# An attention and expert block on one core: gaps between score slots laid out anew, and maxima added to the queries by GpSimd

## The chip, the cores and the metric

The kernel runs on one core of a Trainium2 chip. The metric is the device time of one execution in microseconds (us), as the median of several runs. A core has a matrix engine (TensorE, PE in the profile; its weight loads are shown apart as PEld), a vector engine (VectorE, DVE), a scalar engine (ScalarE, ACT), a general engine (GpSimd, POOL) and a synchronising engine (SyncE, SP), which here issues most of the DMAs. Matmuls write to PSUM, a small memory that ACT and DVE read; everything else is kept in SBUF.

## The reference

The input x is 32 sequences of 512 tokens with 256 channels. The block is an attention with 16 heads of 16 channels, a norm, a layer of experts and another norm.

```
q, k = split(x @ W_attn + b_attn);  v = x, cut into heads
y    = causal_attn(q, k, v)
e    = v[1:] - y[:-1]                    # what the first attention missed
k2   = x[:-1] @ W_k2 + b_k2;  q2 = q[1:]
y2   = causal_attn(q2, k2, e), shifted by one token, first row 0
x1   = layernorm(x + proj(y) + proj(y2))
out  = layernorm(x1 + experts(x1))
```

The experts act on 512 tokens alone, those of the first sequence: two of eight experts each, a gated unit of width 256 and a down projection. For the other 31 sequences the second norm follows the first directly.

## The kernel before

**Groups and steps.** The attention is cut into groups of four heads of one sequence, 4 groups a sequence, 128 in all (`n_all`). `step(n)` works on several groups at once, each at another stage: it takes the row maxima of group n, makes scores and exponentials of group n-2 (first attention, a = 0) and of group n-3 (second attention, a = 1), and values and normalizations of groups n-2 and n-3. The PE queue runs in exactly this order (`manual_schedule`); the other engines' instructions are placed by the framework.

**Slots.** A step has five slots (`units` for the maxima, `banks` for the scores). In a slot, for each of two pairs of heads, `scores` writes one PSUM tile `sc` (L265) and `maxima` one tile `sm` for the other pair (L206, L219), so that the two occupy different rows of the array and overlap. `maxima` first adds a mask: four bf16 matmuls per head (`pick` times `hide`, L206) with 128, 96, 64 and 32 columns in each block, one block in units 0 and 3, two in units 1, 2 and 4; then the products of queries and keys in f32 (L219; each such matmul stands in the trace as two passes). DVE reduces each `sm` to maxima (L230) into one of two `mx` buffers. ACT turns each `sc` into exponentials `pt` (L274, 1024 columns), and GpSimd clears the upper triangle of its diagonal blocks (L278).

**Gaps.** Between slots stand other jobs, by the lists `rest[0]` to `rest[4]` (L493 to L539), run after the slot of that number:

- `augment(n-1)`: transposes the maxima (`mt`, L236); DVE adds them to the queries into `qm` (L240), which the scores of group n-1 read from the next step on.
- `normalize(n-3, 0)` and `normalize(n-3, 1)`: transposes (`yt`, L304), then a maximum with a tiny number, a reciprocal and a product on DVE (L308 to L324), then GpSimd (L321 or L325).
- `values(n-3, 1)` and `values(n-2, 0)`: `av`, L289, over the four key blocks j, then a copy by ACT to `avs` (L297).
- `project(two, m)`: for two groups at once q (m = 0), k (m = 1) or k2 (m = 2): `pj`, L169; ACT adds the bias and writes `pk` (L173); eight DMAs on SP move it into `q_t` or `kk_t` (L184). `pk` has two tags, `half0` and `half1`, with one buffer each.
- once a sequence, `turn` (`ys`, L355, copied by ACT to `ysT`) and `attended` for two halves (`po`, L367, added by DVE to `h`, L374). From the second sequence on `twice_normed` follows on DVE and GpSimd (L389 to L396), and with the second half the store of `h`.

Steps 10 to 17 also carry the experts (`hidden`, `down`).

**PSUM.** All these jobs take their tiles by `bank2` from one pool of four buffers of two banks (L61). They go round in the order in which they are asked for: a tile can be written when the tile four places earlier has been read.

Of the kernel before, what the change touches and what calls it, by code (L numbers as in the profile page):

```python
# [8 lines left out]
F32 = mybir.dt.float32  # L9
# [6 lines left out]
P = 128  # L16
HD = 16
HS = 32
GH = 4
# [8 lines left out]
def block_kernel(  # L28
# [16 lines left out]
    nc = tc.nc  # L45
    B, T, C = x.shape
    NB = T // P
    NC = C // P
    NG = C // (GH * HD)
    E = w_gu.shape[0]  # L50
# [9 lines left out]
    small = ctx.enter_context(tc.tile_pool(name="small", bufs=4))  # L60
# [136 lines left out]
    def maxima(n, u, pair):  # L197
        d = groups[n]
        parts, first, step, kinds = units[u]
        ps = bank2(f"sm{n}_{u}_{pair}")  # L200
        blocks = ps.rearrange("p h (k c) -> p h k c", c=P)
        heads = [(hh, slice(HS * (NH2 * pair + hh), HS * (NH2 * pair + hh + 1))) for hh in range(NH2)]

        for c in range(NB):
            for hh, rows in heads:
                nc.tensor.matmul(  # L206
                    blocks[:, hh, first::step, HS * c :],
                    pick[rows, c],
                    hide[rows, c, kinds[0] : kinds[1], HS * c :],
                    start=(c == 0),  # L210
                    stop=False,
                )
        for i, a, na, at in parts:
            nk = (i + 1) * P
            view = ps[:, :, at * P : at * P + na * nk].rearrange("p h (a k) -> p h a k", k=nk)
            order = [slice(i * P, nk), slice(0, i * P)] if i else [slice(0, P)]
            for keys in order:
                for hh, rows in heads:
                    nc.tensor.matmul(  # L219
                        view[:, hh, :, keys],  # L220
                        d["q"][rows, i * P : (i + 1) * P],
                        d["kk"][rows, a : a + na, keys],
                        start=False,
                        stop=(at == parts[-1][3] and keys == order[-1]),
                    )
        for i, a, na, at in parts:
            nk = (i + 1) * P
            view = ps[:, :, at * P : at * P + na * nk].rearrange("p h (a k) -> p h a k", k=nk)
            to = mx[n % 2][:, i, NH2 * pair : NH2 * (pair + 1), HD + a : HD + a + na]
            nc.vector.tensor_reduce(to, view, AX.X, ALU.max)  # L230

    def augment(n):
        d = groups[n]
        ps = bank2(f"mt{n}")
        for i in range(NB):
            nc.tensor.transpose(  # L236
                ps[:, 0, i * P : (i + 1) * P], mx[n % 2][:, i].rearrange("p h s -> p (h s)"), ident
            )
        d["qm"] = grp.tile([P, T], F32, tag="qm", name=f"qm{n}")
        nc.vector.tensor_add(d["qm"], ps[:, 0], d["q"])  # L240

# [38 lines left out]
    def values(n, a):  # L282
        b, g = divmod(n, NG)
        d = groups[n]
        vals = (v_pad, e_pad)[a]
        ps = bank2(f"av{n}_{a}")
        for j in range(NB):
            for h in range(GH):
                nc.tensor.matmul(  # L289
                    ps[HS * h : HS * (h + 1), 0, j * P :],  # L290
                    vals[:, j, g * GH + h, :],
                    d["pt", a, j, h // NH2][:, h % NH2],
                    start=(j == 0),
                    stop=(j == NB - 1),
                )
        avs = d["avs", a] = work.tile([P, T], F32, tag="avs", name=f"avs{n}_{a}")
        nc.scalar.copy(avs, ps[:, 0])  # L297

    def normalize(n, a):
        b, g = divmod(n, NG)  # L300
        d, s = groups[n], seqs[b]
        ps = bank2(f"yt{n}_{a}")
        for i in range(NB):
            nc.tensor.transpose(ps[:, 0, i * P : (i + 1) * P], d["avs", a][:, i * P : (i + 1) * P], ident)  # L304
        got = ps[:, 0].rearrange("p (n h s) -> p n h s", h=GH, s=HS)
        den = small.tile([P, NB, GH], F32, tag="den", name=f"den{n}_{a}")

        nc.vector.tensor_scalar_max(den, got[:, :, :, HD], 1e-30)  # L308
        rden = small.tile([P, NB, GH], F32, tag="rden", name=f"rden{n}_{a}")
        nc.vector.reciprocal(rden, den)  # L310
        rb = rden.unsqueeze(3).to_broadcast([P, NB, GH, HD])
        cols = slice(g * GH * HD, (g + 1) * GH * HD)

        def heads(t):
            return t[:, :, cols].rearrange("p n (h d) -> p n h d", d=HD)

        if a == 0:
            if g == 0:
                s["y"] = seq.tile([P, NB, C], F32, tag="y", name=f"y{b}")
            nc.vector.tensor_mul(heads(s["y"]), got[:, :, :, 0:HD], rb)  # L320
            nc.gpsimd.tensor_sub(e_pad[:, :, g * GH : (g + 1) * GH, 0:HD], heads(s["xs"]), heads(s["y"]))  # L321
        else:
            y2 = work.tile([P, NB, GH * HD], F32, tag="y2", name=f"y2_{n}")
            nc.vector.tensor_mul(y2.rearrange("p n (h d) -> p n h d", d=HD), got[:, :, :, 0:HD], rb)  # L324
            nc.gpsimd.tensor_add(s["y"][:, :, cols], s["y"][:, :, cols], y2)  # L325
            groups.pop(n)
# [31 lines left out]
    def attended(b, half):  # L358
        s = seqs[b]
        if half == 0:  # L360
            pool = seq if b else const
            s["h"] = pool.tile([P, NB, C], F32, tag="h" if b else "h0", name=f"h{b}")
        ps = bank2(f"po{b}_{half}")
        two = slice(2 * half, 2 * half + 2)
        for i in range(2):
            for c in range(NC):
                nc.tensor.matmul(  # L367
                    ps[:, 0, i * C : (i + 1) * C],
                    s["ysT"][:, c, (2 * half + i) * P : (2 * half + i + 1) * P],
                    wp_sb[:, c],  # L370
                    start=(c == 0),
                    stop=(c == NC - 1),
                )
        nc.vector.tensor_add(  # L374
            s["h"][:, two], ps[:, 0].rearrange("p (i c) -> p i c", c=C), s["xr"][:, two]
        )
        if b:
            twice_normed(b, half)
        elif half:
            norm(s["h"], f"a{b}")  # L380
# [107 lines left out]


    n_all = B * NG  # L490
    first_expert = 2 * NG + 2

    def step(n):  # L493
        ready = lambda k: 0 <= k < n_all
        rest = [[] for _ in units]
        b, r = divmod(n, NG)
        if r == 1 and b + 1 < B:
            load(b + 1)
        if r == 3 and b + 1 < B:
            load_next(b + 1)  # L500
        if ready(n):
            prepare(n)
        if ready(n - 1):
            rest[0].append(lambda: augment(n - 1))
        if ready(n - 3):
            rest[0].append(lambda: normalize(n - 3, 0))
            rest[3].append(lambda: values(n - 3, 1))
            rest[4].append(lambda: normalize(n - 3, 1))
        two = n // 2 + 1
        if ready(2 * two):  # L510
            for m, s in [(0, 4)] if n % 2 == 0 else [(1, 1), (2, 4)]:
                rest[s].append(lambda m=m: project(two, m))
        if ready(n - 2):
            rest[4].append(lambda: values(n - 2, 0))
        b, r = divmod(n - 4, NG)
        if r == NG - 1 and 0 <= b < B:
            rest[2].append(lambda: turn(b))
        b2, r2 = divmod(n - 5, NG)
        if r2 == NG - 1 and 0 <= b2 < B:
            rest[1].append(lambda: attended(b2, 0))  # L520
            rest[2].append(lambda: attended(b2, 1))
        e = n - first_expert
        if e == -1:
            rest[4] += [route, turn_tokens, lambda: load_expert(0)]
        if 0 <= e < E:
            if e + 1 < E:
                load_expert(e + 1)
            rest[1].append(lambda: hidden(e, 0))
            rest[2].append(lambda: hidden(e, 1))
            rest[4].append(lambda: down(e))  # L530
        if e == E:
            rest[4].append(lambda: second_norm(0, moe["acc"]))
        for s in range(len(units)):
            for pair in range(2):
                scores(n - 2, s, 1 - pair)
                if ready(n):
                    maxima(n, s, pair)
            for f in rest[s]:
                f()  # L539
# [2 lines left out]
    load_next(0)  # L542
    for m in range(3):
        project(0, m)
    for n in range(max(n_all + 5, first_expert + E + 1)):
        step(n)


# [71 lines left out]
```

## Time and profile before

| | |
|---|---|
| median of 3 runs | 3240.24 us (3235.77 to 3241.64) |
| the profiled execution: time, span | 3252.37 us, 3250.7 us |
| granted TensorE clock, mean | 0.986 |
| DVE reduces, L230 | 1792 of 916 ns, 1573.6 us |
| ACT exponentials, L274 | 1282 of 1023 ns, 1297.3 us |
| GpSimd selects, L278 | 2048 of 408 ns, 793.1 us |
| ACT copies of av, L297 | 256 of 586 ns |
| ACT pk, L173 | 192 of 688 ns |
| DVE add to qm, L240 | 128 of 680 ns |

Times in the profile are of one execution. A group's line gives its engine, the operation, what it writes and reads, how many there are, their busy time and mean, and the idle time of the engine just before them with what ended it. Since matmuls are pipelined and overlap, the starts of successive matmuls tell more than their durations. [...]

### The profile page before, as it was taken

What the parts mean: (1) busy time and instruction counts of PE and PEld (TensorE: products, weight loads), DVE (VectorE), ACT (ScalarE), POOL (GpSimd) and SP (SyncE); (2) the same over time, 40 slices, a digit from 0 to 9 for tenths busy, and PEclk for the clock granted to TensorE, in tenths of its full rate; (3) what the DMA queues carried; (4) which work ended last, traced back from release to release, by engine and by line L of the source; (5) the groups of instructions that cost most, each with busy time, mean ns of one, the idle gap of its engine ahead of it and who ended that gap; (6) DMA issues with size and microseconds to landing.
All of it is one profiled execution on the core that took longest, in us unless ns stands there. A gap on an engine that the chain in (4) does not pass through costs nothing.

```text
span 3250.7 us, 98094 instructions
## 1 busy us (share of the span) xinstructions
PE 3159.7 (97%) x42312; PEld 2147.1 (66%) x42312; DVE 1999.3 (62%) x3120; ACT 1668.7 (51%) x1823; POOL 1373.8 (42%) x2847
## 2 busy tenths in 40 slices
PE   5999998999999999999999999999999999999997
PEld 4665555667666666666666666676767676676673
DVE  4664444566666666666666666666666666666662
ACT  2554344455555555555555555555555555555554
POOL 4333334344444344444444444444344444443444
PEclk8999999999999999999999999999999999999998
DMA  4111111111111111111111111111111111111110
GB/s 110 37 28 47 37 48 35 39 50 51 32 50 51 41 51 50 50 46 39 50 44 47 50 50 50 39 44 50 40 51 51 49 51 33 50 48 43 38 28 20
DMA packets 144241, 148.13 MB, mean 46 GB/s; under 512 B 40984, under 2 KB 108992, under 8 KB 143808
## 3 DMA queue, kind: packets, MB, share of 16 engines
q1 hardware_dynamic: 143296, 141.42, 16.0%
q8 instruction: 333, 5.46, 0.7%
q14 instruction: 100, 0.82, 0.1%
q10 hardware_dynamic: 416, 0.39, 0.0%
q0 software_dynamic: 96, 0.04, 0.0%
HBM read 74.63 MB, written 16.78 MB: 28 GB/s over the span
## 4 chain that ended last, share of the span: by engine, by line
PE 88%; POOL 5%; DVE 2%; ACT 2%; issue 1%; SPq 1%; DMA 1%; POOLq 0%; DVEq 0%; ACTq 0%
PE sm L219 28%; PE av L289 18%; PE sc L265 14%; PE pj L169 10%; PE sm L206 5%; PE yt L304 4%; POOL h L396 2%; PE mt L236 2%; PE po L367 2%; POOL pt L278 1%; PE gu L450 1%; PE ys L355 1%; PE dn L473 1%; ACT pt L274 1%; POOL r L393 1%
## 5 line engine op out<-in xcount | busy, mean ns | idle before, releaser
L230 DVE TENSOR_REDUCE mx<-sm 128x2 f32<-128x1024 f32 (+3 forms) x1792 | 1573.6, 916 | 965.2 <-PE sm L219 933.0
L274 ACT ACTIVATE pt<-sc 128x1024 f32<-128x1024 f32 (+1 forms) x1282 | 1297.3, 1023 | 683.7 <-PE sc L265 633.6
L219 PE MATMUL sm<-kk_t,q_t 32*128 32x128 f32 (+2 forms) x12288 | 1431.4, 360 | 13.2 <-DMA kk_t<-pk 13.2
L265 PE MATMUL sc<-qm,kk_t 32*128 32x256 f32 (+3 forms) x8192 | 1369.1, 444 | 1.4 <-DVE mx L230 1.2
L278 POOL TENSOR_SCALAR_AFFINE_SELECT pt<-pt 128x256 f32<-128x256 f32 x2048 | 793.1, 408 | 1256.2 <-ACT pt L274 1255.2
L219 PEld LDWEIGHTS sm<-kk_t,q_t 32*128 32x128 f32 x12288 | 920.7, 188 | 35.4 <-issue 8.5
L265 PEld LDWEIGHTS sc<-qm,kk_t 32*128 32x128 f32 x8192 | 711.1, 185 | 224.9 <-issue 134.6
L206 PE MATMUL sm<-hide,pick 32*128 32x128 bf16 (+5 forms) x10240 | 512.3, 217 | 3.8 <-ACT pt L274 3.4
L206 PEld LDWEIGHTS <-pick 32*128 32x128 bf16 x10240 | 368.8, 93 | 32.0 <-issue 12.3
L169 PE MATMUL pj<-xT,wq_sb 128*128 128x512 f32 x768 | 369.7, 604 | 19.8 <-DMA xT<-in_xT 19.8
L297 ACT COPY avs<-av 128x512 f32<-128x512 f32 x256 | 150.1, 586 | 453.3 <-PE av L289 453.3
L289 PE MATMUL av<-pt,e_pad 128*32 128x512 f32 (+3 forms) x4096 | 315.4, 449 | 24.3 <-ACT pt L274 17.2
L289 PE MATMUL av<-pt,v_pad 128*32 128x512 f32 (+3 forms) x4096 | 303.9, 437 | 4.8 <-POOL pt L278 4.8
L173 ACT ACTIVATE pk<-pj,bp_qk 128x512 f32<-128x512 f32 x192 | 132.0, 688 | 337.2 <-PE pj L169 316.4
L289 PEld LDWEIGHTS av<-pt,e_pad 128*32 128x32 f32 x4096 | 134.2, 112 | 243.2 <-issue 139.8
L289 PEld LDWEIGHTS av<-pt,v_pad 128*32 128x32 f32 x4096 | 120.0, 110 | 248.9 <-issue 115.0
L169 PEld LDWEIGHTS pj<-xT,wq_sb 128*128 128x128 f32 x768 | 131.5, 191 | 121.7 <-issue 93.9
L304 PE MATMUL yt<-ident,avs 128*128 128x128 f32 x1024 | 161.4, 280 | 3.8 <-DVE mx L230 2.9
L321 POOL TENSOR_TENSOR e_pad<-xs,y 128x256 f32<-128x256 f32 x128 | 93.4, 730 | 151.2 <-DVE y L320 151.1
L396 POOL TENSOR_SCALAR h<-h,mv,r 128x256 f32<-128x256 f32 x124 | 150.8, 1223 | 6.5
L367 PE MATMUL po<-wp_sb,ysT 128*128 128x256 f32 x512 | 131.4, 401 | 5.7 <-ACT pt L274 4.6
L325 POOL TENSOR_TENSOR y<-y,y 128x256 f32<-128x256 f32 x128 | 93.9, 734 | 90.6 <-DVE y L324 90.6
(76 smaller groups left out, 1405.5 us busy)
## 6 DMA issues: line engine op xcount, KB each, us to landing
kk_t<-pk SPq DMA_DIRECT2D x1024, 32.0 KB
xT<-in_xT SPq DMA_DIRECT2D x32, 512.0 KB
x<-in_x SPq DMA_DIRECT2D x32, 512.0 KB
q_t<-pk SPq DMA_DIRECT2D x512, 32.0 KB
xr<-in_x SPq DMA_DIRECT2D x32, 512.0 KB
out<-h SPq DMA_DIRECT2D x31, 512.0 KB
xs<-in_x SPq DMA_DIRECT2D x32, 384.0 KB
gu<-in_w_gu SPq DMA_DIRECT2D x8, 512.0 KB
```

Of the source, the lines that this page charges most:

```text
L169: nc.tensor.matmul(ps[:, 0], wq_sb[:, m, c, half * P : (half + 1) * P], seqs[b]["xT"][:, c], start=(c == 0), stop=(c == NC - 1))
L206: nc.tensor.matmul(blocks[:, hh, first::step, HS * c :], pick[rows, c], hide[rows, c, kinds[0] : kinds[1], HS * c :], start=(c == 0), stop ...
L219: nc.tensor.matmul(view[:, hh, :, keys], d["q"][rows, i * P : (i + 1) * P], d["kk"][rows, a : a + na, keys], start=False, stop=(at == part ...
L230: nc.vector.tensor_reduce(to, view, AX.X, ALU.max)
L265: nc.tensor.matmul(ps[:, hh, at * P : at * P + nq], d["kk"][rows, a, j * P : (j + 1) * P], d["qm"][rows, j * P :], start=True, stop=True,)
L274: nc.scalar.activation(pt[:, :, lo:hi], ps[:, :, lo:hi], AF.Exp, scale=HD**-0.5)
L278: nc.gpsimd.affine_select(diag, diag, pattern=[[0, NH2], [1, P]], compare_op=ALU.is_ge, fill=0.0, base=-a, channel_multiplier=-1)
L289: nc.tensor.matmul(ps[HS * h : HS * (h + 1), 0, j * P :], vals[:, j, g * GH + h, :], d["pt", a, j, h // NH2][:, h % NH2], start=(j == 0), ...
L297: nc.scalar.copy(avs, ps[:, 0])
L304: nc.tensor.transpose(ps[:, 0, i * P : (i + 1) * P], d["avs", a][:, i * P : (i + 1) * P], ident)
L367: nc.tensor.matmul(ps[:, 0, i * C : (i + 1) * C], s["ysT"][:, c, (2 * half + i) * P : (2 * half + i + 1) * P], wp_sb[:, c], start=(c == 0) ...
L396: nc.gpsimd.tensor_scalar(t[:, i], t[:, i], mv[:, k, 0:1], r[:, k : k + 1], ALU.subtract, ALU.mult)
```

## The change

- In `maxima` the mask matmuls run in the order of blocks 0, 3, 2, 1, that is with 128, 32, 64, 96 columns.
- `augment` goes from the gap after slot 0 to that after slot 3. ACT copies the transposed maxima out of PSUM, and GpSimd adds the queries in place.
- `values` takes its key blocks in the order 0, 2, 1, 3 for a = 0 and 0, 1, 3, 2 for a = 1.
- `normalize` for a = 0 leaves out the maximum with 1e-30.
- `project`: m = 1 after slot 2 of even steps, m = 0 after slot 1 and m = 2 after slot 2 of odd steps (before: m = 0 after slot 4 of even steps, m = 1 after slot 1 and m = 2 after slot 4 of odd steps). The rule for the tag of `pk` is not touched.
- `attended`: the first half after slot 2 of step n, the second after slot 0 of step n+1 (before: after slots 1 and 2 of step n).
- The first expert comes one step later, and the loop has one step more.

```diff
--- before.py
+++ after.py
@@ -201,7 +201,7 @@
         blocks = ps.rearrange("p h (k c) -> p h k c", c=P)
         heads = [(hh, slice(HS * (NH2 * pair + hh), HS * (NH2 * pair + hh + 1))) for hh in range(NH2)]
 
-        for c in range(NB):
+        for c in (0, *range(NB - 1, 0, -1)):
             for hh, rows in heads:
                 nc.tensor.matmul(
                     blocks[:, hh, first::step, HS * c :],
@@ -237,7 +237,8 @@
                 ps[:, 0, i * P : (i + 1) * P], mx[n % 2][:, i].rearrange("p h s -> p (h s)"), ident
             )
         d["qm"] = grp.tile([P, T], F32, tag="qm", name=f"qm{n}")
-        nc.vector.tensor_add(d["qm"], ps[:, 0], d["q"])
+        nc.scalar.copy(d["qm"], ps[:, 0])
+        nc.gpsimd.tensor_add(d["qm"], d["qm"], d["q"])
 
 
 
@@ -284,14 +285,15 @@
         d = groups[n]
         vals = (v_pad, e_pad)[a]
         ps = bank2(f"av{n}_{a}")
-        for j in range(NB):
+        order = [0, 2, 1, 3] if a == 0 else [0, 1, 3, 2]
+        for j in order:
             for h in range(GH):
                 nc.tensor.matmul(
                     ps[HS * h : HS * (h + 1), 0, j * P :],
                     vals[:, j, g * GH + h, :],
                     d["pt", a, j, h // NH2][:, h % NH2],
-                    start=(j == 0),
-                    stop=(j == NB - 1),
+                    start=(j == order[0]),
+                    stop=(j == order[-1]),
                 )
         avs = d["avs", a] = work.tile([P, T], F32, tag="avs", name=f"avs{n}_{a}")
         nc.scalar.copy(avs, ps[:, 0])
@@ -303,11 +305,14 @@
         for i in range(NB):
             nc.tensor.transpose(ps[:, 0, i * P : (i + 1) * P], d["avs", a][:, i * P : (i + 1) * P], ident)
         got = ps[:, 0].rearrange("p (n h s) -> p n h s", h=GH, s=HS)
-        den = small.tile([P, NB, GH], F32, tag="den", name=f"den{n}_{a}")
-
-        nc.vector.tensor_scalar_max(den, got[:, :, :, HD], 1e-30)
         rden = small.tile([P, NB, GH], F32, tag="rden", name=f"rden{n}_{a}")
-        nc.vector.reciprocal(rden, den)
+        sums = got[:, :, :, HD]
+        if a:
+
+            den = small.tile([P, NB, GH], F32, tag="den", name=f"den{n}")
+            nc.vector.tensor_scalar_max(den, sums, 1e-30)
+            sums = den
+        nc.vector.reciprocal(rden, sums)
         rb = rden.unsqueeze(3).to_broadcast([P, NB, GH, HD])
         cols = slice(g * GH * HD, (g + 1) * GH * HD)
 
@@ -488,7 +493,7 @@
 
 
     n_all = B * NG
-    first_expert = 2 * NG + 2
+    first_expert = 2 * NG + 3
 
     def step(n):
         ready = lambda k: 0 <= k < n_all
@@ -501,14 +506,14 @@
         if ready(n):
             prepare(n)
         if ready(n - 1):
-            rest[0].append(lambda: augment(n - 1))
+            rest[3].append(lambda: augment(n - 1))
         if ready(n - 3):
             rest[0].append(lambda: normalize(n - 3, 0))
             rest[3].append(lambda: values(n - 3, 1))
             rest[4].append(lambda: normalize(n - 3, 1))
         two = n // 2 + 1
         if ready(2 * two):
-            for m, s in [(0, 4)] if n % 2 == 0 else [(1, 1), (2, 4)]:
+            for m, s in [(1, 2)] if n % 2 == 0 else [(0, 1), (2, 2)]:
                 rest[s].append(lambda m=m: project(two, m))
         if ready(n - 2):
             rest[4].append(lambda: values(n - 2, 0))
@@ -517,8 +522,10 @@
             rest[2].append(lambda: turn(b))
         b2, r2 = divmod(n - 5, NG)
         if r2 == NG - 1 and 0 <= b2 < B:
-            rest[1].append(lambda: attended(b2, 0))
-            rest[2].append(lambda: attended(b2, 1))
+            rest[2].append(lambda: attended(b2, 0))
+        b3, r3 = divmod(n - 6, NG)
+        if r3 == NG - 1 and 0 <= b3 < B:
+            rest[0].append(lambda: attended(b3, 1))
         e = n - first_expert
         if e == -1:
             rest[4] += [route, turn_tokens, lambda: load_expert(0)]
@@ -542,7 +549,7 @@
     load_next(0)
     for m in range(3):
         project(0, m)
-    for n in range(max(n_all + 5, first_expert + E + 1)):
+    for n in range(max(n_all + 6, first_expert + E + 1)):
         step(n)
```

## The prediction

> **What bounds the kernel now.** I read the page first, then the waits, then the timeline of one undisturbed stretch. The page's first part and its costliest matmul line say TensorE:
>
> ```profile
> PE 3159.7 (97%) x42312; PEld 2147.1 (66%) x42312; DVE 1999.3 (62%) x3120; ACT 1668.7 (51%) x1823; POOL 1373.8 (42%) x2847
> L219 PE MATMUL sm<-kk_t,q_t 32*128 32x128 f32 (+2 forms) x12288 | 1431.4, 360 | 13.2 <-DMA kk_t<-pk 13.2
> ```
>
> The waits of PE between 640 and 3190 us, after the experts, sum to 0.6 us in three lines. So what an edit changes must be a matmul's own time, or a delay inside a slot, where two pairs of heads overlap and a late start leaves no idle mark. The starts of `mt`, one per step, are at 1622.53, 1645.71, 1667.17, 1691.16 and 1716.07: steps of 23.18, 21.46, 23.99 and 24.91 us, 93.54 for four, and the period repeats to 0.01 us. I call them A, B, C, D (n mod 4 = 1, 2, 3, 0; A and C odd).
>
> Inside a slot the sm tile of the first pair runs, then sc of the other pair starts together with the second sm: two sm chains in a row set its length. After a long gap slots take 2.37 (units 0, 3) and 2.60 to 2.63 us (1, 2, 4). Slot 1 takes 3.14 in A, C and D. The timelines of DVE and PE in B show why:
>
> ```profile
> 1644.70 2.36 DVE L230 TENSOR_REDUCE mx<-sm 128x2 f32<-128x1024 f32 x2 [3.65 <-PE sm L219]
> 1646.97 0.68 DVE L240 TENSOR_TENSOR qm<-mt,q_t 128x512 f32<-128x512 f32 x1
> 1647.57 0.17 DVE L308 TENSOR_SCALAR den<-yt 128x16 f32<-128x16 f32 x1
> ...
> 1648.06 0.42 DVE L320 TENSOR_TENSOR y<-yt,rden 128x256 f32<-128x256 f32 x1
> ```
>
> ```profile
> 1646.74 0.70 PE L265 MATMUL sc<-qm,kk_t 32*128 32x512 f32 x2
> 1647.11 0.37 PE L206 MATMUL sm<-hide,pick 32*128 32x256 bf16 x4
> ```
>
> Four PSUM tiles go round in the order of allocation. The sm tile at 1647.11 takes the place of slot 0's last, whose reduce ended at 1647.06; the second sm waits for `yt`, read until 1648.48. By such comparison the slots lose 0.76, 0.95, 0.55 and 0.52 us in A to D, 2.78 per four steps, some 89 us in all. That is all that moving gaps can win.
>
> [...]the first L219 of a chain takes 0.35 us against 0.27 for its like, for its load begins only with the last, 27 ns long, L206. [...]Here the semaphore moves 1.37 us after the end of the last issue (median of 192 batches). [...]here 1309 ns (L464, 128x512) against 680 (L240).
>
> **The change, part by part.**
>
> Order of the pick matmuls. With widths 128, 32, 64, 96 the last[...] is a wide one. In units 1, 2, 4 (two blocks) starts were 117, 80, 54 ns apart, then 109 to the load's end; now 117, 27, 54, 109: 53 saved. In units 0, 3: 63, 41, 27, 109 become 63, 25, 27, 109: 16 saved. Two chains a slot: 2 x (3 x 53 + 2 x 16) = 382 ns a step, on PE's path, 48.9 us over 128 steps.
>
> Gap after slot 0. `mt` (0.49) and the qm add leave; `yt` stays, 0.53. Now slot 1's first sm waits for the exp of slot 0's second sc, which ends 0.88 after slot 0 (1646.59 against 1645.71): a loss of 0.37 in B, C, D. In A the moved `po` (1.9) covers it.
>
> Slots 1 and 2 adjoin in B and D: DVE needs 2 x (0.96 + 0.42) per slot, PE now 2.5. Stepping the ring through gives 0.20 and 0.17 more, 0.74 each. Slot 3 has a projection before it and loses nothing. Slot losses become 0 + 0.74 + 0.37 + 0.74 = 1.85.
>
> Gaps. PE's work in them is the same, but runs between slots go from 17 to 18 per four steps and neighbours change; adding the pieces (0.53, 1.91, 1.81, 1.02, 2.82 and so on) gives 40.76 against 40.29. Sum: 4 x (12.59 - 0.38) + 1.85 + 40.76 = 91.45, or 2.09 less per four steps; over 31.25 such periods 65 us gained.
>
> Evictions. `qm` costs ACT a copy (586 ns by L297) and GpSimd 1309 ns; both sit in the gap after slot 3 (2.82 with av), 5 us before scores read qm. Should that cover fail, each us late costs PE one, but I find 2.5 to spare. Behind GpSimd's add stand the selects of slot 4, which values reads; by L278 they end 1.6 after slot 4, and with `yt` and j = 0, 2 first, values asks for j = 1 at 1.8. Order of j, the dropped max (164 ns), two more waits of av: nothing, between 0 and 0.1 us a step.
>
> The projections. m=0 and m=2 of one `two` write the same single pk buffer, tag half of (two+m)%2. Before, a step lay between them. Now m=0 stands after slot 1, m=2 after slot 2 of an odd step; m=2's ACTIVATE must wait until eight DMAs have read m=0's pk. ACT and SP in the middle, and the only place where before met this wait, its start (ACT and SP):
>
> ```profile
> 1617.98 0.69 ACT L173 ACTIVATE pk<-pj,bp_qk 128x512 f32<-128x512 f32 x1 [1.66 <-PE pj L169]
> ```
>
> ```profile
> 1618.69 4.93 SPq L184 DMA_DIRECT2D q_t<-pk  x8
> ```
>
> ```profile
> 25.41 0.69 ACT L173 ACTIVATE pk<-pj,bp_qk 128x512 f32<-128x512 f32 x1 [1.08 <-PE pj L169]
> 35.28 0.69 ACT L173 ACTIVATE pk<-pj,bp_qk 128x512 f32<-128x512 f32 x1 [9.19 <-DMA q_t<-pk]
> ```
>
> From the start of m=0's ACTIVATE: 0.71 to the first issue, 5.39 for eight (mean for q_t; 4.93 is the least), 1.37 to land: 7.5. PE brings m=2 there after 1.91 + 2.49 = 4.40. So ACT stands 3.1 us; queued behind are ysT in C, two exps, the qm copy and avs. PE goes on for three tiles; the fourth, slot 3's second sm, reuses pj's bank. It had about 0.3 to spare (ACTIVATE ends 2.71 after pj's start, the sm is due 3.05), so PE loses 2.75. In A, SP's order puts the store of h before these DMAs; h now comes from the po after slot 0: DVE till 4.3 after that slot, GpSimd 3.5 more (L392 to L396), store at 7.9, ACTIVATE's end at 7.6. With 0.4 for the issue, 0.7 more: 3.45. Over 31 periods 192 us, less 8 where `gu` lies between (four odd expert steps, 1.9 each): 184. Bounds: with least issue span and no store 2.3 each, 140; with the issue hiccups of over 1 us, 240. I take the mean since every issue counts.
>
> The clock. In these stops PE is idle 1.6 to 2.4 us. Among the experts it has such stops already; the windows view shows what follows (last columns of interest: PE busy first, PEclk after the five engines):
>
> ```profile
> 268.00:272.70 4.70, 2.21 (x27) 1.08 (x21) 3.56 (x5) 4.37 (x5) 2.32 (x2) 1.00 0.38 112
> 272.70:276.20 3.50, 3.50 (x24) 1.41 (x28) 0.00 (x0) 0.77 (x1) 0.97 (x3) 0.51 0.02 5
> ```
>
> The values matmuls then took 4.05 instead of 2.36. Of 14 idle times of 1.0 to 2.9 us between 200 and 640 us, 11 were followed by a half clock for 3.4 or 6.8 us, at about 1.8 us lost each. So 62 x 0.79 x 1.8 = 88 us; bounds 0 (no drop) and 62 x 3.4 = 211 (always two windows).
>
> The expert stage starts a step later with its stops at other tiles: unknown, -15 to +15, taken as 0. The longer loop adds no work.
>
> **Sum.** -65 + 184 + 88 = +207 against the profiled execution's 3252.4: 3459. That execution lies 12 above the median of the runs, 3240, which gives 3447; I say 3445.
>
> **Rivals.** (1) The clock holds: the stops of A and C are no emptier than those three of 14 that passed. Then 3240 - 65 + 184 = 3359. (2) Faster: pk is free in time. Mechanism: the wait for the landing at L173, priced 0 instead of 184 (and no idle, so no clock); it decides from 4.7 us on, the 4.40 plus the spare 0.3. Then 3240 - 65 = 3175. Against it stand 7.5 from three durations and the 9.19 at the start. (3) GpSimd becomes late as well: selects held by the 1.3 us add delay values by 0.5 in each of 127 steps, 64 more: 3509. Against: it is 42% busy and mostly waits for ACT; for: its spare at values is 0.2 to 0.6.
>
> **How the numbers follow.** Forecast 0.56, rival 1 0.28, rival 3 0.10, rival 2 0.06. The forecast's spread is 3390 to 3500 from 140 to 240 and the clock's share; the range reaches down to rival 1 with a smaller stop and up to rival 3: 3330 to 3505. Some 0.2%, 6 us, can be told from no change. Slower is all but rival 2: 0.94; faster 0.05; same 0.01.
>
> **What would show it.** ACT's pk waits for DMA q_t<-pk some 62 times, about 3 us each; PE's sm L206 of unit 3 waits for ACT pk; odd steps grow to about 26 to 29 us while B and D shrink to 21.0 and 22.9; the mean clock falls to 0.93 to 0.96. The first L219 falls towards 0.30 and slot 1 to 2.9. Wrong would be: no such wait, or q_t landing within 4.7 us of the ACTIVATE.

## The result, and the profile after

| | before | after |
|---|---|---|
| median | 3240.94 us (4 runs) | 3523.32 us (4 runs, 3521.42 to 3531.66) |
| ratio | | 1.088, interval 1.086 to 1.090 |
| profiled execution: time, span | 3252.37, 3250.7 us | 3521.42, 3519.7 us |
| granted TensorE clock, mean | 0.986 | 0.945 |

The kernel became 8.8% slower. The direction and the wait were forecast, but the time lies 78 us above the forecast's 3445 and 18 above the upper end of its range.

The page of after: first the busy times, then the group of the projection's ACTIVATE (operation, shapes, number | busy us, mean ns | idle time before it and what ended most of it). Below them, lines of the waits (engine, instruction <- releaser: us in total, times, longest).

```profile
PE 3286.0 (93%) x42312; PEld 2078.3 (59%) x42312; DVE 1882.2 (53%) x2864; ACT 1724.7 (49%) x1955; POOL 1533.2 (44%) x2975
...
L173 ACT ACTIVATE pk<-pj,bp_qk 128x512 f32<-128x512 f32 x192 | 131.9, 687 | 487.6 <-DMA q_t<-pk 302.1
```

```profile
ACT pk L173 <- DMA q_t<-pk: 302.1, 60, 10.7
...
PE sm L206 <- ACT pk L173: 91.5, 30, 6.7
...
PE sc L266 <- ACT pk L173: 53.7, 28, 3.2
```

In before, the wait at L173 was there twice. Now it comes 60 times, about 5 us each, and TensorE waits for the same ACTIVATE 58 times. TensorE waits 145 us in these two lines, yet 282 were lost, and TensorE's *busy* time rose by 126 although it does the same number of matmuls. The second fact points to the clock.

One stop of kind A shows the chain: the timelines of ACT, SP and PE (start, us, instruction; in brackets the idle time before it and what ended it).

```profile
1838.84 0.69 ACT L173 ACTIVATE pk<-pj,bp_qk 128x512 f32<-128x512 f32 x1 [1.03 <-PE pj L169]
1839.99 2.05 ACT L275 ACTIVATE pt<-sc 128x1024 f32<-128x1024 f32 x2 [0.47 <-POOL h L401]
1847.85 0.69 ACT L173 ACTIVATE pk<-pj,bp_qk 128x512 f32<-128x512 f32 x1 [5.81 <-DMA q_t<-pk]
```

```profile
1839.96 0.41 SPq L403 DMA_DIRECT2D out<-h  x1
1840.46 5.83 SPq L184 DMA_DIRECT2D q_t<-pk  x8
```

```profile
1844.26 1.02 PE L266 MATMUL sc<-qm,kk_t 32*128 32x512 f32 x4
1848.59 0.45 PE L206 MATMUL sm<-hide,pick 32*128 32x128 bf16 x8 [3.31 <-ACT pk L173]
1848.81 2.07 PE L219 MATMUL sm<-kk_t,q_t 32*128 32x128 f32 x8
1850.81 1.11 PE L236 MATMUL mt<-ident,mx 128*128 128x128 f32 x4
1851.86 3.75 PE L291 MATMUL av<-pt,e_pad 128*32 128x512 f32 x32
```

m=0's `pk` is ready at 1839.53. The store of h stands ahead of it on SP, so the issue of the eight DMAs begins at 1840.46 and ends at 1846.29; m=2's ACTIVATE starts at 1847.85. TensorE has then been idle for 3.31 us, because the next `sm` needs the PSUM tile which that ACTIVATE reads. The windows view cuts the same step at the changes of the clock (columns: us, busy us of PE, PEld, DVE, ACT and POOL with counts, PEclk, DMA share, GB/s):

```profile
1829.86:1845.28 15.42, 15.42 (x192) 9.93 (x189) 10.20 (x16) 7.33 (x8) 10.66 (x18) 1.00 0.28 80
1845.28:1847.89 2.61, 0.00 (x0) 0.00 (x0) 0.42 (x1) 0.04 (x1) 0.00 (x0) 1.00 0.32 60
1847.89:1848.59 0.70, 0.00 (x0) 0.00 (x0) 0.00 (x0) 0.70 (x2) 0.00 (x0) 0.50 0.48 155
1848.59:1854.72 6.13, 6.13 (x36) 2.65 (x39) 1.23 (x1) 2.36 (x3) 2.09 (x3) 0.50 0.35 103
1854.72:1860.93 6.21, 6.21 (x112) 4.04 (x104) 3.28 (x7) 2.64 (x3) 1.99 (x5) 1.00 0.01 3
```

The clock halves 2.6 us after TensorE fell idle, before it resumes, and the next 6.13 us of work run at half speed: from start to start, `mt` takes 1.04 us here and 0.59 in experiment 1, `av` 3.68 and 2.29. So the wait is paid twice.

The mean length of a step, from the start of slot 0 to the next, over the same 94 steps after the experts (the last two columns are the experiments 1 and 4 below):

| step | before | after | m=2 in another buffer | after with filler |
|---|---|---|---|---|
| A | 23.18 | 30.67 | 23.88 | 28.31 |
| B | 21.45 | 21.06 | 21.05 | 21.08 |
| C | 24.00 | 28.91 | 23.51 | 26.54 |
| D | 24.91 | 22.88 | 22.88 | 22.88 |
| four steps | 93.53 | 103.52 | 91.31 | 98.81 |
| half clock in these steps, us | 0 | 266 | 0 | 14 |

### The profile page after: what moved, and what is told of

It is laid out like the page before. It is cut to its first block, busy times and chain, and to the rows that moved or that the text cites. A ratio compares the mean times of both kernels' runs of the same rounds, so it can differ in the third digit from the quotient of the medians.

```text
span 3519.7 us, 97633 instructions
## 1 busy us (share of the span) xinstructions
PE 3286.0 (93%) x42312; PEld 2078.3 (59%) x42312; DVE 1882.2 (53%) x2864; ACT 1724.7 (49%) x1955; POOL 1533.2 (44%) x2975
## 4 chain that ended last, share of the span: by engine, by line
PE 76%; DMA 3%; ACT 1%; POOL 1%; issue 1%; DVE 0%; SPq 0%; ACTq 0%; POOLq 0%; DVEq 0%
PE sm L219 22%; PE av L291 17%; PE sc L266 14%; PE pj L169 9%; PE sm L206 4%; PE yt L306 4%; DMA q_t<-pk 3%; PE po L372 3%; PE mt L236 3%; ACT pk L173 1%; PE ys L360 1%; ACT pt L275 0%; SPq L184 0%; POOL h L401 0%; ACTq L173 0%
## 5 line engine op out<-in xcount | busy, mean ns | idle before, releaser
L230 DVE TENSOR_REDUCE mx<-sm 128x2 f32<-128x1024 f32 (+3 forms) x1792 | 1557.9, 916 | 1299.1 <-PE sm L219 1297.8
L219 PE MATMUL sm<-kk_t,q_t 32*128 32x128 f32 (+2 forms) x12288 | 1413.4, 358 | 7.3 <-DMA kk_t<-pk 7.3
L219 PEld LDWEIGHTS sm<-kk_t,q_t 32*128 32x128 f32 x12288 | 932.1, 190 | 33.0 <-issue 7.4
L206 PE MATMUL sm<-hide,pick 32*128 32x128 bf16 (+5 forms) x10240 | 518.2, 218 | 103.0 <-ACT pk L173 91.5
L169 PE MATMUL pj<-xT,wq_sb 128*128 128x512 f32 x768 | 389.0, 630 | 29.0 <-DMA xT<-in_xT 19.7
L206 PEld LDWEIGHTS <-pick 32*128 32x128 bf16 x10240 | 312.0, 93 | 162.6 <-issue 153.7
L291 PE MATMUL av<-pt,e_pad 128*32 128x512 f32 (+3 forms) x4096 | 393.3, 535 | 15.4 <-POOL pt L279 6.5
L173 ACT ACTIVATE pk<-pj,bp_qk 128x512 f32<-128x512 f32 x192 | 131.9, 687 | 487.6 <-DMA q_t<-pk 302.1
L241 POOL TENSOR_TENSOR qm<-qm,q_t 128x512 f32<-128x512 f32 x128 | 163.0, 1274 | 92.4 <-ACT qm L240 82.4
L306 PEld LDWEIGHTS yt<-ident,avs 128*128 128x128 f32 x1024 | 107.3, 141 | 87.0 <-ACT pt L275 65.3
```

The lines of the kernel that those rows point to most:

```text
L169: nc.tensor.matmul(ps[:, 0], wq_sb[:, m, c, half * P : (half + 1) * P], seqs[b]["xT"][:, c], start=(c == 0), stop=(c == NC - 1))
L173: nc.scalar.activation(pk, ps[:, 0], AF.Identity, bias=bp_qk[:, m, half : half + 1])
L206: nc.tensor.matmul(blocks[:, hh, first::step, HS * c :], pick[rows, c], hide[rows, c, kinds[0] : kinds[1], HS * c :], start=(c == 0), stop ...
L219: nc.tensor.matmul(view[:, hh, :, keys], d["q"][rows, i * P : (i + 1) * P], d["kk"][rows, a : a + na, keys], start=False, stop=(at == part ...
L241: nc.gpsimd.tensor_add(d["qm"], d["qm"], d["q"])
L291: nc.tensor.matmul(ps[HS * h : HS * (h + 1), 0, j * P :], vals[:, j, g * GH + h, :], d["pt", a, j, h // NH2][:, h % NH2], start=(j == orde ...
```

## The experiments

Each ratio is to runs of before made beside the experiment; their medians are 3245 to 3250 us.

**1. The shared buffer taken away.** In after:

```diff
-        pk = work.tile([P, T], F32, tag=f"half{(two + m) % 2}", name=f"pk{two}_{m}", bufs=1)
+        pk = work.tile([P, T], F32, tag=f"half{(two + min(m, 1)) % 2}", name=f"pk{two}_{m}", bufs=1)
```

> The changed kernel with one thing altered: projection m=2 writes the buffer of m=1 and no longer that of m=0, so that its ACTIVATE (L173) finds a buffer that was read a step earlier. Theory (the wait for the landing of the eight q_t DMAs, and the half clock after it, are all that is lost): the waits of ACT pk for DMA q_t<-pk fall from 302 us to under 20, steps of kind A and C fall from 30.7 and 28.9 to about 24, B and D stay at 21.1 and 22.9, the clock is 0.985 or more, and the time is the prediction's sum without its two losses, 3240 - 65 = 3175 (3150 to 3200). Rival (the new qm on ACT and GpSimd, or the new gaps, cost as well): over 3260, with A and C above 25 though no wait for the landing is left.

Measured: 3184.82 us, ratio to before 0.981 (0.978 to 0.984), clock 0.984; A and C 23.88 and 23.51. The rival falls: with the wait gone nothing of the loss is left, and the rest of the change is a gain of 1.9%. One expectation missed. The waits still show a line of that name:

```profile
ACT pk L173 <- DMA q_t<-pk: 62.7, 50, 1.3
```

It can't be the old wait: m=2's ACTIVATE now starts 4.46 us after m=0's in C, when the eight DMAs are still being issued. It is most likely the wait for `pj`, put down to an event that happened to come last.

**2. The positions of the projections alone.** In before:

```diff
-            for m, s in [(0, 4)] if n % 2 == 0 else [(1, 1), (2, 4)]:
+            for m, s in [(1, 2)] if n % 2 == 0 else [(0, 1), (2, 2)]:
```

> The kernel before with one thing altered: the projections stand where the changed kernel has them (m=1 after slot 2 of an even step, m=0 after slot 1 and m=2 after slot 2 of an odd one), the buffers' rule untouched; mask order, gaps, qm and attended are the old ones. Theory (the two projections that share a buffer are what costs): some 62 waits of ACT pk for DMA q_t<-pk of 3 to 5 us, a clock near 0.945, and 3240 + 62 x (2.8 to 3.1 of stop + 2.6 of half clock) = 3575 to 3595; the range 3520 to 3620. Rival (the move alone does little, it takes the new gaps or qm with it): 3230 to 3300.

Measured: 3728.68 us, ratio 1.147 (1.143 to 1.151), clock 0.938: above the range that the theory gave. A and C grew to 28.59 and 28.92, as in after. But D grew as well, from 24.91 to 31.64, for which the theory had no reason. GpSimd in such a step:

```profile
1922.35 0.78 POOL L278 TENSOR_SCALAR_AFFINE_SELECT pt<-pt 128x256 f32<-128x256 f32 x2
1927.47 2.34 POOL L350 TENSOR_TENSOR xr<-xr,bp 128x1024 f32<-128x1024 f32 x1 [4.34 <-DMA xr<-in_x]
1929.76 0.41 POOL L278 TENSOR_SCALAR_AFFINE_SELECT pt<-pt 128x256 f32<-128x256 f32 x1
```

The add to `xr` waits 4.34 us for its load and then takes 2.34; the selects behind it on GpSimd are what `values` waits for. SP in this step, and below it SP in a D of before:

```profile
1916.11 5.92 SPq L184 DMA_DIRECT2D kk_t<-pk  x8
1922.43 0.41 SPq L398 DMA_DIRECT2D out<-h  x1
1922.88 0.52 SPq L349 DMA_DIRECT2D xr<-in_x  x1
```

```profile
1702.60 0.40 SPq L349 DMA_DIRECT2D xr<-in_x  x1
1707.77 0.41 SPq L398 DMA_DIRECT2D out<-h  x1
```

In before the load goes out 5 us ahead of the store; here the DMAs of m=1 are in its way, and it comes behind both. Whether this is a loss of its own, or a result of the first, was open.

**3. The positions, without the shared buffer.** The edits of 1 and 2 together, in before.

> The kernel before with two things altered: the projections stand where the changed kernel has them, and m=2 writes the buffer of m=1, so that the wait for the landing of the q_t DMAs is gone. In the run with the positions alone (old buffers) steps of kind D also took 31.6 instead of 24.9, with av waiting 6.5 us for GpSimd, which waited for the load of xr behind the eight kk_t DMAs of m=1. Theory (that is a second loss of its own, which the changed kernel escapes because its second half of `attended` stands a step later): A and C back at about 23.5 to 24, D still at 31 to 32, and 3240 + 31 x 6.7 = 3448 (3400 to 3480). Rival (the load of xr was late only because the whole queue had been pushed back by the wait): D at 24 to 25 and 3225 to 3250.

Measured: 3465.31 us, ratio 1.068 (1.065 to 1.071). A and C are back at 24.02 and 24.04, D stays at 31.69:

```profile
PE av L289 <- POOL pt L278: 156.2, 37, 6.4
POOL xr L350 <- DMA xr<-in_x: 153.9, 31, 21.2
```

So it is a loss of its own. In after that line is

```profile
POOL xr L355 <- DMA xr<-in_x: 25.4, 4, 23.7
```

and D takes 22.88. The second half of `attended`, with the store of h and the reuse of `xr` behind it, stands a step later there; in experiment 1 the load goes out 5.5 us into A, when SP has nothing else to issue, and GpSimd finds it landed (it waits for that load 4 times in the whole run, 23.7 us in all and 21.7 of them at once, where experiment 3 has 31 waits and 153.9). By the traces this detail of the change pays for the projection's new place; no run moved `attended` alone.

**4. TensorE kept busy during the wait.** In after, behind the matmuls of `project`; twelve matmuls of no use, which take 2.7 us from the first start to the next matmul's:

```diff
+        if m == 2 and two > 10:
+            for _ in range(12):
+                nc.tensor.matmul(ps[:, 1], pick[:, 0], pick.rearrange("p n c -> p (n c)"), start=True, stop=True)
```

> The changed kernel plus work of no use: right behind projection m=2, from the eleventh pair of groups on (53 of them, after the experts), twelve bf16 matmuls of 128 x 512, [...]whose result nothing reads. They keep TensorE busy while ACT waits for the landing and change nothing of the wait. Theory (a stop costs its 3 us and then some 2.6 more because the clock falls): the waits of ACT pk stay at some 300 us, the filler takes the place of the idle time, the half clock after the experts goes, and 53 x 2.6 = 138 us are won: about 3385 (3350 to 3430), clock 0.97 or more. Rival 1 (the stop alone costs all of it): 3523. Rival 2 (the filler adds to the path):[...].

Measured: 3394.67 us, clock 0.985: more work, and 129 us less time. PE's timeline and ACT's wait in this run (the added lines move L173 to L176):

```profile
1786.56 1.98 PE L169 MATMUL pj<-xT,wq_sb 128*128 128x512 f32 x4
1788.38 2.75 PE L174 MATMUL pj<-pick 128*128 128x512 bf16 x12
...
1793.96 0.33 PE L209 MATMUL sm<-hide,pick 32*128 32x128 bf16 x8 [0.76 <-ACT pk L176]
```

```profile
ACT pk L176 <- DMA q_t<-pk: 239.3, 48, 10.4
```

The ACTIVATE of m=2 comes no earlier (8.78 and 7.69 us after m=0's in A and C, 8.72 and 7.65 in after, means after the experts). What went is the half clock, from 266 to 14 us in the 94 steps. This splits the loss per stop. There are 47 stops in those steps; A and C together took 59.58 in after, 54.85 with filler and 47.39 without the wait: (54.85 - 47.39) / 2 = 3.73 us are the stop, (59.58 - 54.85) / 2 = 2.36 the clock. In C the filler covers the whole wait, so it could itself be what is left there; but with half of it, in the next experiment, C takes 26.71 against 26.54.

**5. Half the filler.** `range(6)` for `range(12)`.

> The changed kernel plus six matmuls of no use behind projection m=2 instead of twelve (1.25 us, by the 2.5 that twelve took): the idle time of TensorE in the stops falls from 1.4 to 3.5 us to some 0.3 to 2.2. The 60 idle times of the changed kernel after the experts say: none of 6 below 1 us was followed by a half clock, 15 of 18 from 1 to 2 us, 36 of 36 above 2. Theory (the length of the idle time decides): about half of the 53 stops keep their half clock, mostly one window of 3.4 us, and the time lies between 3395 and 3523, at 3440 to 3485. Rival 1 (any stop sets it off, whatever its length): 3510 to 3525. Rival 2 (a busy array at the start of the wait is enough): 3390 to 3405.

Measured: 3454.11 us (3441.35 to 3463.09); the six took 1.4 us, not 1.25. C came down to 26.71, A stayed at 30.39. From 840 us on 18 idle times of 0.3 us and more are left in C, 0.88 us in the mean, and 2 of them were followed by half clock; in A 25 of 1.90 us, and 24 were. So the length of the idle time decides, not that there is one.

The records say how. The 70 half-clock periods of after all start on one grid of 3413.33 ns, none more than 3 ns off, and 67 of them last one or two cells of it. I laid that grid over five runs (after and the experiments 2, 4, 5 and 8, each from 840 us on) and counted TensorE's idle time in each cell at full clock:

| idle share of the cell | cells | next cell at half clock |
|---|---|---|
| under 0.2 | 3311 | 0 |
| 0.2 to 0.35 | 46 | 6 |
| 0.35 to 0.5 | 83 | 61 |
| over 0.5 | 142 | 140 |

By this table the odds pass one half at some 1.3 us of idle time in one cell, an estimate: 6 of 46 cells dropped at a share of 0.2 to 0.35 (0.7 to 1.2 us), 61 of 83 at 0.35 to 0.5 (1.2 to 1.7 us). An idle time of 2.7 us holds that much wherever it falls on the grid, and all 66 of that length in these runs were followed by half clock. The way back stays open: of 260 cells at half clock without any idle time, 69 were followed by another one.

**6. The order of the mask alone.** In before:

```diff
-        for c in range(NB):
+        for c in (0, *range(NB - 1, 0, -1)):
```

> The kernel before with one thing altered: the four blocks of the mask are written in the order 0, 3, 2, 1 (L204). Theory (the load of the first q weights is covered by a wide last mask matmul): 382 ns less a step, 48.9 us less in all: 3191 (3180 to 3210), first L219 of a chain about 0.30 instead of 0.35. Rival (the slot's length is set by something else than these two chains): 3240 within 10.

Measured: 3206.45 us, ratio 0.987 (0.985 to 0.990), 39 us less and not 49. A chain became shorter by just what was worked out, 1138 to 1084 ns with two blocks and 801 to 784 with one (median from the first L206 to the last L219). But slot 1, which waits for DVE here, went only from 3.14 to 3.10, and slot 3 stayed at 2.40 in C and D, where it follows `ys` and `po`, so a step gains 0.28 instead of 0.38.

**7. qm made by VectorE again.** In the kernel of experiment 1:

```diff
-        nc.scalar.copy(d["qm"], ps[:, 0])
-        nc.gpsimd.tensor_add(d["qm"], d["qm"], d["q"])
+        nc.vector.tensor_add(d["qm"], ps[:, 0], d["q"])
```

> The changed kernel with m=2 in the buffer of m=1 (3185 us), and besides with qm made by VectorE again, in one addition straight from PSUM; its place after slot 3 stays. Theory (ACT and GpSimd do the new qm beside other work and nothing waits for VectorE there, so the move of qm is worth nothing either way): 3175 to 3195. Rival 1 (VectorE is late for the maxima of slot 4 with 0.68 us more in that gap): up to 0.4 us a step, 3195 to 3235. Rival 2 (the copy and the add delay the exps or the selects): down to 3150.

Measured: 3187.08 us against 3184.82, four steps 91.32 against 91.31. The maxima added by GpSimd behind a copy, which give the change its name, are worth nothing either way.

**8. The store of h issued by GpSimd.** In after:

```diff
-            nc.sync.dma_start(out[b].rearrange("(n p) c -> p n c", p=P), t)
+            nc.gpsimd.dma_start(out[b].rearrange("(n p) c -> p n c", p=P), t)
```

> The changed kernel with the store of h (in twice_normed) issued by GpSimd and no longer by SP, ahead of whose q_t DMAs it stood in steps of kind A. Theory (the store holds the first q_t DMA back by 0.94 us in A against 0.03 in C): the distance from m=0's ACTIVATE to m=2's falls in A from 8.85 to about 7.8, C stays at 7.65, and 30 x 0.9 to 1.4 us are won: 3480 to 3497. Rival (the store is not what holds it, or GpSimd pays for the issue): 3515 to 3535.

Measured: 3496.37 us, at the upper end of what was expected. The first q_t DMA now follows the ACTIVATE by 0.07 us instead of 0.94 in A, but the eight took 5.66 instead of 5.45 and the distance fell only from 8.72 to 8.11. (The 8.85 of the expectation has one step with an expert in its mean.) A went from 30.67 to 29.24, C rose from 28.91 to 29.43.

**9. The buffers as they are, m=2 one gap later.** In after:

```diff
-            for m, s in [(1, 2)] if n % 2 == 0 else [(0, 1), (2, 2)]:
+            for m, s in [(1, 2)] if n % 2 == 0 else [(0, 1), (2, 3)]:
```

> The changed kernel, its buffers as they are, with projection m=2 after slot 3 of an odd step, behind mt and av, and not after slot 2. m=2 then comes 1.9 + 2.5 + 2.4 + 0.6 + 2.3 = 9.7 us after m=0 in A and 0.97 more in C, against the 8.85 and 7.65 that the landing took. Theory (it is the distance in time between the two writers of one buffer that decides): no stop after the experts, clock 0.98 or more, 3185 and some 10 for slots 2 and 3 that adjoin in A: 3185 to 3205. Rival (the shared buffer costs at any distance within a step): over 3300.

Measured: 3186.74 us, ratio 0.982 (0.980 to 0.984), clock 0.989. m=2's ACTIVATE comes 10.0 us after m=0's in A and 10.7 in C, and no stop is left after the experts. The two projections may share the buffer, if the second comes later than the 7.65 and 8.72 us that the first one's DMAs need.

**10. A faster version.** In the kernel of experiment 1, m=1 after slot 1 of an even step:

```diff
-            for m, s in [(1, 2)] if n % 2 == 0 else [(0, 1), (2, 2)]:
+            for m, s in [(1, 1)] if n % 2 == 0 else [(0, 1), (2, 2)]:
```

> The changed kernel with m=2 in the buffer of m=1 (3185 us), and besides with projection m=1 after slot 1 of an even step instead of slot 2, so that slots 1 and 2 no longer adjoin in B and D. Theory (slots that adjoin pay for it: 5.56 us for the two against 2.74 + 2.50 with a projection between them): 0.32 less in D; in B, where slots 2 and 3 adjoin instead, about 0.1 less; 31 x 0.42 = 13 us: 3172 (3165 to 3180). Rival (the load of xr comes behind the eight DMAs of m=1 earlier and holds GpSimd up, or the projection's ACTIVATE delays an exp): 3185 or more.

Measured: 3168.55 us (3163.25 to 3171.51), ratio 0.976 (0.974 to 0.978), the fastest of all. The time was met, its reason was not. Four steps fell from 91.31 to 91.13 only, 6 us over the kernel; in D slots 1 and 2 took 5.24 us instead of 5.56, but the projection and `po`, no longer side by side, took 0.2 more. In the profiled runs 17 us came before the first of the 94 steps, and the half clock of the whole run is 76 us instead of 103. Why fewer stops of the expert stage fell to half clock was not followed up.

## Why the prediction came out low

**Gain of 65.** The sum held. Experiment 1 has the change without its wait: 61 us less than before in both spans (3250.7 to 3189.2), four steps 91.31 where 91.45 was worked out. B and D were forecast at 21.0 and 22.9 and took 21.06 and 22.88. In part this is luck: the slots of four steps take 50.0 us there, 0.7 less than worked out, and the gaps 41.3, 0.6 more. The pieces also make 93.43 of before's 93.54, so they give 62 by themselves. `qm` at nothing was right (experiment 7), and GpSimd's lateness (rival 3) did not come: `av` waits 8.4 us for GpSimd in all of after, 8.6 in before.

**The landing wait, 184.** The mechanism was right: m=2's ACTIVATE waits for m=0's eight DMAs, 60 times, and PE stops at the fourth tile. In A that is slot 3's second `sm`, as forecast; in C, where `ys` takes a tile as well, it is the second `sc`. The size was low: 3.73 us a stop against a mean of 3.1, by experiment 4 4.43 in A and 3.03 in C, where 3.45 and 2.75 stood. From ACTIVATE to ACTIVATE it took 8.72 us in A, where 8.2 was worked out, and 7.65 in C against 7.5. The store of h held the first DMA back by 0.92 us, not 0.7, and the ACTIVATE starts 0.25 us after the last semaphore has moved, which the sum put at nothing; the landing, 1.38 us after the last issue in the median of both kernels, and the issues, 5.45 and 5.22 us against 5.39, were about as read. The rest is the spare 0.3 us: m=2's ACTIVATE is 4.26 us later in A than in experiment 1, and TensorE loses 4.43; in C it is 3.19 and 3.03. So of the spare nothing was left in A and half in C.

**The clock, 88: the step that failed.** The prediction multiplied 62 stops by a chance of 0.79 and by 1.8 us, both counted from 14 stops among the experts. Neither carried over. From 840 us on all 50 stops of after were followed by half clock. A stop cost 2.36 us by this, not 0.79 x 1.8 = 1.42. That the stops were longer than forecast is not the reason: the idle time of TensorE is 3.04 us in the mean in A but 1.95 in C, inside the forecast's 1.6 to 2.4, and C dropped in 25 of 25 cases too and lost as much (28.91 - 26.54 = 2.37). What differs from the sample is also how long the half clock lasts: two cells after 33 of the 50 stops, after 4 of the 11 in the sample. Why it lasts longer after the experts stays open. Rival 1, that the clock holds, had 0.28 and was 164 us off.

**The sum.** The prediction's +207 in the profiled execution is +269 in spans. In the 94 steps the clock's term is short by 47 x 0.94 = 44 us and the stop's by 47 x 0.63 = 30. The 15 stops outside them cost 44 us together (the spans of after and experiment 1 differ by 330.5, of which 286 lie in the 94 steps), where the prediction had 15 x 4.5 - 8 = 60: 16 back. With the gain 4 smaller this is the 62. The other 16 of the 78 us lie in the step from the profiled execution to the median: the forecast took off 12 because that of before lies above its median, and 2 by rounding, but that of after lies 2 below its own.

**The range.** It let the clock's share run only with the forecast's own spread, and its upper end, 3505, even lies below rival 3's 3509, up to which it was said to reach. The bound of two cells at every stop, 211 us, stood in the text and would have held the time.

## What to carry over

When a change moves two users of a single-buffered tile together, work out the time from the first write to the last read's landing, DMA by DMA and with all that stands ahead on the queue, and compare it with the new distance; a place one gap later (experiment 9, 3186.74 us) or another buffer's name (experiment 1, 3184.82 us) was all it took here. Price a stop of the matrix engine twice, once for itself and once for the clock (3.73 and 2.36 us here): count how much idle time falls into one cell of the grid that the clock's records show (3413 ns here) rather than take a rate from another stage. And when a sum of edits loses, try it without the one that waits before giving up the rest: here the rest was a gain of 1.9%.

## What was not expected of the hardware

- Idle time in a part of a cell was enough to halve the clock. On the grid of 3413.33 ns a cell with more than half of its time idle was followed by half clock in 140 of 142 cases, one with less than a fifth in none of 3311.
- Work of no use made the kernel 3.7% faster than after (3394.67 against 3523.32 us), since it kept the clock up (14 us of half clock in the 94 steps instead of 266) during a wait that it did not shorten (from ACTIVATE to ACTIVATE 8.78 us in A against 8.72).
- One load issued behind eight small DMAs and a store (experiment 3) made D 6.8 us longer than in before, an estimate of 210 us over 31 such steps, half clock included: GpSimd stood 4.5 us for it in the median, and every select behind it was late.
